# One transformer layer with experts on one core: TensorE transposes for batch 0, weight loads one head ahead, a ring of one-row gathers, a running sum on VectorE, and batch 1 prepared later

## The chip, the cores and the metric

The kernel runs on one core of a Trainium2 chip. The core has five engines, each with its own instruction queue: PE (TensorE, matmuls), DVE (VectorE), ACT (ScalarE), POOL (GpSimd) and SP (SyncE, which here only issues DMAs). POOL issues DMAs as well. The engines wait for each other and for DMAs through semaphores; within one queue, instructions start in order. The time is the device time of one execution in microseconds.

## The reference

There are B = 4 sequences of S = 512 rows with D = 512 columns. A small cross attention is added first, then a layer with causal attention of 16 heads and a mixture of experts (top 6 of 16, 352 wide) with a shared expert (704 wide).

```python
# cross attention: the keys and queries come from ctx, the values are layernorm(x)
query = einsum('bnc,dc->bnd', ctx, Wq) + bq ; key = einsum('bnc,dc->bnd', ctx, Wk) + bk
attention = softmax(einsum('bnd,bmd->bnm', query, key))
x = x + einsum('bln,bmn->blm', layernorm(x), attention)
# the layer, on hidden = layernorm(x)
h = rmsnorm(hidden, ln1_w); q, k, v = h @ wq, h @ wk, h @ wv      # 16 heads of 128
attn = softmax(causal(q k^T / sqrt(128)))
x1 = hidden + (attn v) @ wo
t = rmsnorm(x1, ln2_w)
probs = softmax(t @ gate_w.T); topv, topi = top_k(probs, 6); topv /= sum(topv)
routed = sum over the six of topv * (silu(t @ eg_w) * (t @ eu_w)) @ ed_w
shared = (silu(t @ sg_w.T) * (t @ su_w.T)) @ sd_w.T
out = x + layer output, where the layer output is x1 + routed + shared
```

## The kernel before

Most products are made of three fp16 products. `split` (lines 72 to 74) makes a high half with ACT (L73) and the rest, the low half, with DVE (L74); `mm3` (L80 to 88) issues hi by hi, hi by lo and lo by hi into one PSUM bank (source lines L83, L86, L87). A product of two fp32 operands thus costs three matmuls and two splits. PSUM has eight banks, given out by tag: "a" three, "s" three, "w" two.

`flip` (L90) is a DMA transpose issued on SP. It turns the normalised cross attention (`pn` into `ptp`, for `xm`) and the normed rows (`hh` into `hT`, for queries, keys and values), 128 rows at a time. `after` (L93) makes one instruction stand behind another on its queue, without a wait of its own on the chip. Apart from these, a scheduler decides the order of each queue from the program order, the dependences and its own timing model.

*The cross attention* of batch b is the generator `xattn(b)` (L204 to 363). It loads the context, x and its transpose (batches 0 and 1 on SP, later ones on POOL), and then yields between small steps: projections `xq`, energies `en`, softmax (`pm`, then split into `pn`), `flip` into `ptp`; `stats` (L250) for the row norms, `center` (L266), which subtracts the mean on POOL; per row tile the product `xm`, its addition to the centred rows (L337), the statistics of the result, its power -1/2 on POOL (L347), `hu`, the split `hh`, and `flip` into `hT`. A call of `step(b, n)` runs n steps. The driver (L370 to 390) runs batch 0 to its end, then the loads of ln2 and of the gate, then nine steps of batch 1. Where PE would stand idle in batch 0, `warm` fills it with 22 matmuls that nobody reads.

*The attention* runs over a list of 64 pairs (batch, head), in groups of two heads (HG = 2): four heads of batch 0, then groups of batches 0 and 1 by turns, so that two batches share a loaded weight, and then the same with batches 2 and 3. In each turn of the loop (L780 to 841) head n is prepared (`queries`, `values`, then `scores`), and the head one turn behind is finished (`attend`: the softmax goes through a flip `pt` on SP, then `av`; `project`: `wo` and the residual). Steps of the next batch's cross attention are issued in between, for batch 1 two in each of the first six turns. For the first head `queries` and `values` first run on half of the rows (L790 to 794), since the first half of `hT` lands earlier.

*Weights* come through `fetch` (L407 to 434). At first use the fp32 weight is loaded into a staging tile (`wqk_st`, `wv_st`, `wo_st`; two buffers), split by ACT and DVE, used, and its fp16 form written to DRAM at once (L429). In later batches the fp16 form is loaded (L414) when the head is issued. These DMAs are on POOL, except for the first ones.

*The routing* of a batch (`route2`, L532) has softmax, top 6 and, over the 16 experts, a running sum in four doublings (L578 to 582), with the copies on DVE and the additions on POOL. `scatter` (L456 to 475) writes rows into expert order, 96 indirect DMAs on POOL (L467), paced by `pace`, a copy on POOL that waits for an attention result.

*The experts* (L1119 to 1219) run one by one: gate and up (`g`, `u`), `hf` and its low half on DVE, down (`y`), and a store `y_d`. As soon as rows have all six results, POOL gathers them (L1169) and DVE adds them, weighted, to `acc` (L1178). The gathered rows land in a tile `yg` of three rows, of which there are two; `lookahead(tile, 3, 4)` (L1197) sets this up, with up to four gathers kept in flight. Before the last stage `gather_all(0)` (L1212) waits until none is in flight, and further tiles are taken from another pool.

## Time and profile before

| what | us |
|---|---|
| runs | 1768.77, 1769.27, 1786.13 |
| median of the runs | 1769.27 |
| the profiled execution | 1762.41 |
| its span | 1760.7 |
| PE busy | 1708.6 |
| DVE, ACT, POOL busy | 1116.2, 829.3, 485.1 |

The profiled execution took 6.9 us less than the median. The span is the part from the first to the last recorded event. PE is busy in 97% of it. Three views are needed to read it: the list of an engine's waits, with what ended them; a queue's timeline, one line to an instruction or a run of like ones, with the idle time ahead of it in brackets; and windows, one line to a stretch, with each engine's busy time and instruction count, the granted TensorE clock (1.00 is full speed), the DMA share and the rate.

The page's list of DMA issues gives the time from issue to landing, for instance:

```profile
y_d<-yt SPq DMA_DIRECT2D x96, 256.0 KB, 2.8
wqk<-wqk_d POOLq DMA_DIRECT2D x20, 512.0 KB, 5.0
wqk_d<-wqk POOLq DMA_DIRECT2D x15, 512.0 KB, 4.0
wqk_st<-in_wqk_dram POOLq DMA_DIRECT2D x14, 512.0 KB, 6.4
```

The columns are the transfer, the queue, its count, the size of one, and the median time to landing.

### The profile page before, as it was taken

Reading aid. Unit: us, or ns where it says so; the run is one execution under the profiler, and the core shown is the slowest. Engines: PE = TensorE matmul, PEld = TensorE weight load, DVE = VectorE, ACT = ScalarE, POOL = GpSimd, SP = SyncE. Lnnn points to the kernel's source line nnn. Section 1 sums busy time; section 2 is a strip of 40 time slices with the busy share of each in tenths; the row PEclk is TensorE's granted clock in tenths of the full one; section 3 lists DMA queues with packets and bytes.
Section 4 is the critical chain, followed back from the end, with each engine's and each line's share of the span. In section 5 each row is a group of like instructions: output and inputs, shape, how many; then the busy total and the mean of one; then the engine's idle time right before and its main releaser. Section 6 shows DMA issues by size and latency. Waiting matters only on the chain. (4 is left out here: it accounts for less than half of the span.)

```text
span 1760.7 us, 27659 instructions
## 1 busy us (share of the span) xinstructions
PE 1708.6 (97%) x9919; PEld 932.9 (53%) x9919; DVE 1116.2 (63%) x2766; ACT 829.3 (47%) x1711; POOL 485.1 (28%) x614
## 2 busy tenths in 40 slices
PE   7899999999998999999999999999999999999998
PEld 3555556565654555556555544455555555555553
DVE  6787877787785676776667647544434344356755
ACT  4565655565643545454445422344544445444431
POOL 5524212240255242121113454300000000034654
PEclk9999999999999999999999999999999999999999
DMA  7787867575687787556547653755554546589866
GB/s 246 181 205 184 225 150 192 122 196 118 138 183 187 163 177 179 120 120 118 111 104 132 140 155 128 247 173 148 150 173 137 154 143 163 154 228 254 221 198 213
DMA packets 392212, 296.24 MB, mean 168 GB/s; under 512 B 334880, under 2 KB 335136, under 8 KB 391296
## 3 DMA queue, kind: packets, MB, share of 16 engines
q1 hardware_dynamic: 353360, 159.87, 39.9%
q0 software_dynamic: 38704, 134.51, 25.5%
q8 instruction: 80, 1.31, 0.3%
q14 instruction: 68, 0.56, 0.1%
HBM read 124.81 MB, written 88.94 MB: 121 GB/s over the span
## 5 line engine op out<-in xcount | busy, mean ns | idle before, releaser
L1169 POOL DMA_INDIRECT yg<-y_d,yrc x96 | 109.9, 1145 | 505.2 <-PE u L87 426.0
L673 ACT ACTIVATE pe<-pe,bnm 128x128 f32<-128x128 f32 (+3 forms) x256 | 142.5, 557 | 161.5 <-DVE bnm L671 161.3
L83 PE MATMUL qk<-hT,wqk 128*128 128x512 f16 (+1 forms) x520 | 196.4, 378 | 9.1 <-DMA wqk<-wqk_d 5.5
L86 PE MATMUL qk<-hT,wqk 128*128 128x512 f16 (+1 forms) x520 | 196.5, 378 | 0.0
L87 PE MATMUL qk<-hT,wqk 128*128 128x512 f16 (+1 forms) x520 | 196.3, 377 | 0.0
L74 DVE SCALAR_TENSOR_TENSOR pn<-pe,brc,pn 128x128 f16<-128x128 f32 (+3 forms) x256 | 148.1, 590 | 21.3 <-ACT pn L73 18.0
L671 DVE CUSTOM_DVE_ANT_0 pe<-sc,causal 128x128 f32<-128x128 f32 (+3 forms) x256 | 117.0, 485 | 66.9 <-PE sc L668 65.9
L73 ACT ACTIVATE pn<-pe,brc 128x128 f16<-128x128 f32 (+3 forms) x256 | 133.5, 553 | 34.1 <-ACT pe L673 17.8
L83 PE MATMUL v<-wv,hT 128*128 128x256 f16 x512 | 139.8, 273 | 0.9 <-DMA hT<-hh 0.9
L87 PE MATMUL v<-wv,hT 128*128 128x256 f16 x512 | 139.7, 273 | 0.0
L86 PE MATMUL v<-wv,hT 128*128 128x256 f16 x512 | 139.7, 273 | 0.0
L83 PE MATMUL g<-xT,wt 128*128 128x384 f16 (+2 forms) x384 | 127.3, 331 | 0.0
L86 PE MATMUL g<-xT,wt 128*128 128x384 f16 (+2 forms) x384 | 127.2, 331 | 0.0
L87 PE MATMUL g<-xT,wt 128*128 128x384 f16 (+2 forms) x384 | 127.2, 331 | 0.0
L1058 ACT ACTIVATE hT_e<-hf 128x384 f16<-128x384 f32 (+3 forms) x96 | 51.1, 532 | 133.6 <-DVE hf L1072 133.2
L83 PE MATMUL y<-dt,hT_e 128*128 128x512 f16 (+1 forms) x288 | 109.4, 380 | 0.0
L87 PE MATMUL y<-dt,hT_e 128*128 128x512 f16 (+1 forms) x288 | 108.9, 378 | 0.0
L86 PE MATMUL y<-dt,hT_e 128*128 128x512 f16 (+1 forms) x288 | 108.9, 378 | 0.0
L73 ACT ACTIVATE qkt<-qk 128x512 f16<-128x512 f32 x128 | 75.1, 587 | 70.7 <-PE qk L87 70.5
L705 DVE SCALAR_TENSOR_TENSOR x<-wo,x 128x512 f32<-128x512 f32 x128 | 87.2, 685 | 33.3 <-PE wo L87 32.9
L467 POOL DMA_INDIRECT xs_d<-h2p,slotu x96 | 98.7, 1028 | 28.3 <-issue 27.1
L74 DVE SCALAR_TENSOR_TENSOR qkt<-qk,qkt 128x512 f16<-128x512 f32 x128 | 87.5, 684 | 18.3 <-ACT qkt L73 15.2
(333 smaller groups left out, 4041.5 us busy)
## 6 DMA issues: line engine op xcount, KB each, us to landing
y_d<-yt SPq DMA_DIRECT2D x96, 256.0 KB, 2.8
est<-in_ew_dram SPq DMA_DIRECT2D x32, 704.0 KB, 6.2
est<-in_ed_dram SPq DMA_DIRECT2D x16, 768.0 KB, 4.7
wqk<-wqk_d POOLq DMA_DIRECT2D x20, 512.0 KB, 5.0
wqk_d<-wqk POOLq DMA_DIRECT2D x15, 512.0 KB, 4.0
wqk_st<-in_wqk_dram POOLq DMA_DIRECT2D x14, 512.0 KB, 6.4
xs_d<-causal POOLq DMA_DIRECT2D x16, 384.0 KB, 5.6
wv<-wv_d POOLq DMA_DIRECT2D x10, 512.0 KB, 5.7
```

What stands on the lines that cost most here:

```text
L73: return (nc.scalar.activation(hi, src, AF.Copy, scale=scale), nc.vector.scalar_tensor_tensor(lo, src, scale, hi, ALU.mult, ALU.subtract))
L74: nc.vector.scalar_tensor_tensor(lo, src, scale, hi, ALU.mult, ALU.subtract))
L83: ins = nc.tensor.matmul(o, lh, rh, start=start and j == 0, stop=False)
L86: nc.tensor.matmul(o, lh, rl, start=False, stop=False)
L87: ins = nc.tensor.matmul(o, ll, rh, start=False, stop=stop and j == n - 1)
L467: ins = nc.gpsimd.indirect_dma_start(out=xs_d, out_offset=bass.IndirectOffsetOnAxis(ap=slotu[:, tt, k:k + 1], axis=0), in_=h2ps[tt], in_of ...
L671: nc.vector.tensor_tensor_reduce(pe, ps[:, :w], causal[:, S - w:], -1.0, 3e38, ALU.add, ALU.min, nm)
L673: nc.scalar.activation(pe, pe, AF.Exp, bias=nm, scale=-1.0, accum_out=sm)
L705: nc.vector.scalar_tensor_tensor(x2[:, t, :], ps, 1.0 / (VS * WS), x2[:, t, :], ALU.mult, ALU.add)
L1058: nc.scalar.activation(hT[:R, ic, :w], hf, AF.Copy)
L1169: nc.gpsimd.indirect_dma_start(out=yg, out_offset=None, in_=src, in_offset=bass.IndirectOffsetOnAxis(ap=idx[:, tt, k:k + 1], axis=0))
```

## The change

1. *Transposes.* A new helper `swap` multiplies four 128x128 blocks of the high half by an fp16 identity (`id16`) into one PSUM bank, then four of the low half into another; ACT copies the first bank out, and DVE (for `ptp`) or ACT (for `hT`) the second. Batch 0 uses it in place of `flip`. Batches 1 to 3 keep `flip`.
2. *Batch 0's start.* x is loaded ahead of its transpose. `center` is on ACT for batch 0. `warm` issues 12 matmuls in place of 22. The first two `xm` products are computed in four column pieces, each as soon as its part of `ptp` is there; the other two take "s" banks. The driver stops batch 0 after eleven steps; the rest of it (`second_half`: its last two row tiles, the loads of ln2 and gate, five steps of batch 1) comes after the first half of the first head. The second head's weight `wqk1` is fetched there too.
3. *Batch 1.* It goes on by four steps in each of the first six turns, except turn 1, in place of two. Its transposed x (`xT32`) is loaded into the "wo" buffers of the weights and not into the staging buffers.
4. *Weights.* In each turn the loads of the next head's fp16 weights (`wqk`, `wv`, and `wo` after `attend`) are issued at the end of the preparation, if the weight has been seen before. Write-backs are kept in a list and issued behind the staging load of a later weight. `pace` also stands behind the last such load.
5. *Running sum.* The four additions go to DVE.
6. *Gathers.* A ring of seven tiles of one row, with five gathers kept in flight, takes the place of two tiles of three. The `hs` tiles of the shared expert get a pool of their own, which closes before the experts; the last batch's lie in the experts' weight staging. The call before the last stage has no argument, so it doesn't wait for gathers in flight.

```diff
+    def swap(o, i, tag, low):
+        done = []
+        for a, put in enumerate((nc.scalar.copy, low)):
+            ps = bank(tag, "swap")
+            for c in range(C):
+                j = (a * C + c) * P
+                nc.tensor.matmul(ps[:, c * P:(c + 1) * P], i[:, j:j + P], id16, start=True, stop=True)
+            done.append(put(o[:, a * C:(a + 1) * C, :], ps.rearrange("p (c q) -> p c q", c=C)))
+        return done
...
-            t = (stg if b else wg).tile([P, 1024], F32, tag="st" if b else "wo", name="xT32")
+            t = (stg if b > 1 else wg).tile([P, 1024], F32, tag="st" if b > 1 else "wo", name="xT32")
...
+            if b == 0:
+                zz["center"] = nc.scalar.activation(xt[:, t, :], xt[:, t, :], AF.Identity, bias=nb[:, t:t + 1])
+                after(zz["center"], zz["calm"][0])
+                return
             nc.gpsimd.tensor_scalar(xt[:, t, :], xt[:, t, :], nb[:, t:t + 1], None, ALU.add)
...
-            zz["ptp", b] = flip(ptp[:, :, ml], pn)
+            if b:
+                flip(ptp[:, :, ml], pn)
+            else:
+                zz["third"] = zz["calm"][1] if m else None
+                zz["calm"] = swap(ptp[:, :, ml], pn, "a", nc.vector.tensor_copy)
...
-            warm(22, last)
+            warm(12, last)
...
+        early_xm = [bank("w", f"xm{b}_{t}") for t in range(0 if b else 2)]
+        for m in range(NT):
+            ml = slice(m * P, (m + 1) * P)
+            for t, ps in enumerate(early_xm):
+                tl = slice(t * P, (t + 1) * P)
+                zz["xm", b, t] = mm3(ps[:, ml], [(lnp[:, c, tl], lnp[:, C + c, tl], ptp[:, c, ml], ptp[:, C + c, ml])
+                                                 for c in range(C)])
+        if b == 0:
+            early_xm += [product(t, "s") for t in range(2, NT)]
...
-            zz["hT", b] = flip(hT[b][:, :, tl], hh)
+            if b:
+                flip(hT[b][:, :, tl], hh)
+            else:
+                zz["cast"] = swap(hT[b][:, :, tl], hh, "as"[t // 2], nc.scalar.copy)[1]
...
-    step(0, 99)
+    step(0, 5 + 6)
...
+    def second_half():
+        step(0, 99)
+        after(zz["low", "wqk1"], zz["hh", 0])
...
+        step(1, 5)
...
-    step(1, 1 + 2 * NT)
...
+        w = soon.pop(nm, None)
+        if w is None:
+            w = pool.tile([P, 2, n], F16, tag=tag, name=f"{nm}_{b}")
+            if nm in seen:
+                zz["load"] = nc.gpsimd.dma_start(w.rearrange("p a n -> p (a n)"), scr)
+        if early:
+            soon[nm] = w
+            return
...
+            save(0, None if nm == "wqk1" else ins)
...
+    def save(keep, behind=None):
+        while len(unsaved) > keep:
+            scr, w = unsaved.pop(0)
+            zz["pad"] = nc.gpsimd.dma_start(scr, w.rearrange("p a n -> p (a n)"))
+            if behind:
+                after(zz["pad"], behind)
...
-            nc.gpsimd.tensor_tensor(nx[:, :, sft:], cs[:, :, sft:], cs[:, :, :E - sft], ALU.add)
+            nc.vector.tensor_tensor(nx[:, :, sft:], cs[:, :, sft:], cs[:, :, :E - sft], ALU.add)
...
+            if n + 1 < NH:
+                b, h = heads[n + 1]
+                wqk_of(b, h, True)
+                if h % HG == 0:
+                    wv_of(b, h // HG, True)
...
+                wo_of(b, h // HG, True)
...
-            step(1, 2)
+            step(1, 4 * (n != 1))
...
-    lookahead(lambda: st2.tile([P, 3, D], F32, tag="hs", name="yg"), 3, 4)
+    hctx.close()
+    ring_p = ctx.enter_context(tc.tile_pool(name="ring", bufs=RING, side="right", reuse_waits="tile"))
+    lookahead(lambda: ring_p.tile([P, 1, D], F32, name="yg"), 1, RING - 2)
...
-    gather_all(0)
+    gather_all()
```

## The prediction

> **What bounds the kernel now.** I read the page's busy shares first, then what TensorE (PE) waited for, then the timelines of the queues that feed each wait.

> ```profile
> PE 1708.6 (97%) x9919; PEld 932.9 (53%) x9919; DVE 1116.2 (63%) x2766; ACT 829.3 (47%) x1711; POOL 485.1 (28%) x614
> ```
> ```profile
> PE av L83 <- DMA pt<-pn: 16.9, 10, 3.9
> PE xm L83 <- DMA ptp<-pn: 9.8, 2, 5.8
> PE qk L83 <- DMA wqk<-wqk_d: 5.5, 1, 5.5
> PE u L1081 <- DVE hf L1072: 3.9, 2, 2.1
> PE qk L83 <- DMA hT<-hh: 3.6, 2, 3.2
> ```
> The columns are total us, times, longest. PE is the bound: of a span of 1760.7 us it lacks 52.1. The change leaves the products alone, so it can only take from these 52.1 us, from matmuls run at a lower clock, and from the few matmuls that it adds or drops. The listed waits make 39.7 of the 52.1; smaller ones and some 8 us behind the last matmul are the rest.

> ```profile
> 25.64 0.58 PE L83 MATMUL xm<-ptp,lnp 128*128 128x512 f16 x1 [5.82 <-DMA ptp<-pn]
> 26.02 0.63 PE L86 MATMUL xm<-ptp,lnp 128*128 128x512 f16 x1
> 26.45 0.63 PE L87 MATMUL xm<-ptp,lnp 128*128 128x512 f16 x1
> ...
> 548.81 0.61 PE L83 MATMUL qk<-hT,wqk 128*128 128x512 f16 x1 [5.51 <-DMA wqk<-wqk_d]
> 549.21 0.63 PE L86 MATMUL qk<-hT,wqk 128*128 128x512 f16 x1
> 549.64 0.63 PE L87 MATMUL qk<-hT,wqk 128*128 128x512 f16 x1
> ...
> 1626.41 0.32 PE L1081 MATMUL u<-xT,wb 128*128 128x384 f16 x1 [2.13 <-DVE hf L1072]
> 1626.57 0.32 PE L1082 MATMUL u<-xT,wb 128*128 128x384 f16 x1
> ```
> Columns: start, us, engine, line, operation, the idle time before it and what ended it. Behind the waits of 5.82 and 5.51 us the 512-column matmuls follow each other every 0.43 us; elsewhere it is 0.2155. This lasts some 3.2 us, so such a wait costs about 1.6 us more. Behind the 2.13 us there is no such stretch. The granted clock says the same by window:

> ```profile
> 540.00:560.00 20.00, 14.49 (x75) 7.54 (x74) 9.10 (x28) 6.36 (x16) 9.39 (x13) 0.83 0.75 172
> 560.00:580.00 20.00, 20.00 (x126) 11.95 (x125) 13.37 (x36) 7.80 (x18) 9.37 (x13) 1.00 0.90 220
> ```
> Last, the queues behind the waits:
> ```profile
> 16.77 7.28 SPq L91 DMA_TRANSPOSE ptp<-pn  x4
> 24.16 8.16 POOL L267 TENSOR_SCALAR xt<-xt,nb 128x512 f32<-128x512 f32 x4 [0.88 <-DVE nb L262]
> 538.93 0.96 POOL L467 DMA_INDIRECT xs_d<-h2p,slotu  x1 [0.30 <-issue]
> 539.89 0.60 POOL L414 DMA_DIRECT2D wqk<-wqk_d  x1
> 150.91 0.22 PE L666 MATMUL sc<-qkt,qkt 128*128 128x128 f16 x1
> 150.97 0.22 PE L667 MATMUL sc<-qkt,qkt 128*128 128x128 f16 x1
> ```

> **The change part by part.** All sums are against the profiled execution, 1762.41 us, of which 1760.7 is span; the median shown is 1769.27, 6.9 above it, and I carry the saving over to the median unchanged. "Work" is PE time counted at full clock in queue order (0.2155 us for 512 columns, pro rata below).

> 1. Swaps in batch 0. Eight tiles by eight 128-column matmuls are 64; the two `sc` lines above follow each other by 0.054 to 0.06 us: 64 x 0.054 = 3.45 us. Ten warm matmuls go: -2.16. Net +1.29 of PE. [...]

> 2. The start of batch 0. Before, the four flips end at 24.05, the first `xm` starts at 25.64, POOL centres rows until 32.32, and the first `v` starts at 40.74. After, each `ptp` part waits for its PSUM copies; three DVE copies at about 0.6 (the ScalarE copy of 128x512 from PSUM is 0.59) put the last at about 24. The first two `xm` need only their last quarter then (24 matmuls of 0.054), so they are there at 25.3, all four by 30.5. Centring on ACT starts at 26.3 (`nb` behind POOL's power and two staged splits) and takes four times about 0.6. DVE then has for two row tiles: xt 1.3, statistics 1.2, small ones 0.6, hu 1.3, hh 1.4: from 26.9 to 32.8. Swap and copy add 1.2 to 1.7: first `v` at about 34.5. Rows 2 and 3 follow by the same list at 42.5, where before `hT` landed at 51.32. Then `xq1` waits for the low half of the next context (DVE, about 47), and `qk0_1_0` starts at about 52.1 with 38.4 of work done: 13.7 lost. Before it starts at 58.89 with 39.65 done: 19.2 lost. Difference 5.5, less the 1.29: **-4.2**. Moving x's load ahead of xT's is booked at nothing: ACT reads xT behind 10.82; 0 to +1.

> 3. Batch 1 a step later. `xm1_0` has 77 us of work ahead of it in place of 53, and its four flips stand on SP long before: the wait of 3.97 at 76.60 and its slow stretch go, **-5.6**. Small waits around it (0.67, 0.25) go too, -0.9. In exchange, work between the last `xm1` and the first `qk1_4` falls from 10.67 to 8.41. In the trace that chain (DVE list, POOL's power, hh, flip) took 11.25, with 0.39 waited; by DVE's order after it is about 9.0 of DVE and 3.1 from hh to landing, 12.1. So 3.7 are waited, 3.3 more. Here the clock decides: the trace has half clock after 3.23 and none after 2.48. [...] I take the rows: 1.6, together **+4.9** (0 to +6). What is late is queued as follows: on PE everything behind `qk1_4_0` stands.

> 4. Heads. The room between a head's last `sc` and its `av` falls for av1_5 from 17.0 to 12.5 us of work, for av0_13 from 16.6 to 13.7, rises for av1_1 from 9.2 to 11.8, and falls for av1_3 from 11.2 to 9.6. The waits of 1.58 (av1_1) and 2.48 (av1_3) so trade places: 0, with -6 to +4. Batches 2 and 3 keep theirs. (Room is counted in both queue orders, as work is.)

> 5. Weight loads ahead. The load that PE awaited at 548.81 was issued at 539.89, behind ten scatters; in the new order it precedes all of them. 5.51 and 1.5 of slow matmuls go: **-7.0** (-4 if it lands late by the wait of its buffer). Most other loads keep their place in POOL's order. Write-backs behind the staging loads: nothing waits for them but later batches, 0.

> 6. Running sum on DVE: four adds a batch, 0.15 to 0.4 us each by the small DVE rows; PE has heads in front of it there and waits for no route: 0 (0 to +1).

> 7. Ring of seven rows. The two waits of `u` for `hf` (DVE held by an add whose row was late, 1.95 at 1623.47) sum to 3.9; a gather now waits for the add seven rows back, before at times four. I book **-3.5** (-4 to 0). Changed `hs` buffers and the last stage without its drain: PE never waits there, 0.

> Sum: -4.2 - 5.6 - 0.9 + 4.9 - 7.0 - 3.5 = **-16.3**: 1746.1 for the profiled execution, 1753.0 for the median.

> **The rivals.** *All of it comes.* `hT` of batch 1 lands in time, as in the trace within 0.39: 5 less, and av waits in batches 0 and 1 (1.90, 1.58, 2.48) vanish: 6 less; 1742 to 1748. For it: the trace chain held beside a busier DVE. Against: 2.3 us of cover are gone.

> *Given back.* The start of batch 0 moves only from DMA to DVE and ACT, whose copies and splits I placed from lists and not from a trace: part 2 gives 0, and the hT wait is 5: 1760 to 1765. For it: DVE is 13.5 to 16 of 20 us busy there already.

> *Slower: ACT held by staged weights.* POOL issues 29 staging loads (14 `wqk`, 8 `wo`, 7 `wv`), landing in about 6 us. ACT already waits 26.1 us for them (9.9, 9.2 and 7.0 by its list of waits), up to 3.78 at 175.67; a softmax held there shows as the 1.90 of av1_5. With less room (part 4) and heads starting 10 us earlier the whole 26.1 could reach PE: 24 more, 1777. From 16.3 of the 26.1 on, the kernel is slower than before. Against it: so far 1.9 of it arrives, and batch 1's xT leaves the staging buffers. [...]

> That the change doesn't do what it says holds in part: the loads "ahead" mostly wait for the same buffers. If the one at 548.81 does too, 1760.

> **How the numbers follow.** Forecast 1753 (1748 to 1760): 0.45. All comes: 0.25. Given back: 0.18. Slower: 0.12, half of it beyond 1%. One per cent, 17.7 us, is about what a measurement of this kernel can tell from no change; it lies at 1751.6, inside the forecast's own range, of which I put 0.17 below. Faster 0.25 + 0.17 = 0.42; slower 0.06; within 0.52. The range leaves out the slower rival and the last of the gains: 1740 to 1767.

> **What would show it.** First `v` near 34.5 and `qk0_1_0` near 52; no wait of `xm` for `ptp`; no wait for `wqk_d`; a new wait of `qk1_4` for `hT` of 3 to 4 us with half clock behind it; `u` without waits for `hf`. The forecast is wrong if waits for `hT` or `pt` sum to more than 25, or if swaps follow each other at over 0.1 us.

## The result, and the profile after

The changed kernel takes 1794.38 us (median; 1782.19 to 1796.64), the kernel before beside it 1772.14. The ratio is 1.0138 [1.0104, 1.0172]: about 24 us slower by the ratio (22 by the medians), where 16 less were forecast. Two later series of the same kernel gave 1.0056 [1.0031, 1.0082] and 1.0119 [1.0076, 1.0163]. The sign holds in all three; the size is anything from 10 to 24 us.

The busy shares of the changed kernel (busy us, share of the span, instructions):

```profile
PE 1721.8 (96%) x10045; PEld 942.0 (53%) x10045; DVE 1124.0 (63%) x2787; ACT 835.3 (47%) x1727; POOL 487.5 (27%) x594
```

PE is 13.2 us busier than before, yet the 126 matmuls that were added are short ones (64 swaps; `xm` in quarters; ten warm ones fewer). Counted by columns at full clock, PE's work is 1678.1 us against 1676.8, the 1.3 more that the prediction booked. Most of the rest of the busier PE is half clock: by the distance between back-to-back matmuls 22.7 us go to it, 14.2 before. The remainder of the span is waiting. What PE waited for, in the changed kernel (total us, times, longest):

```profile
PE av L84 <- DMA pt<-pn: 21.9, 8, 7.0
PE qk L84 <- DMA hT<-hh: 8.8, 1, 8.8
PE u L1167 <- DVE hf L1158: 7.6, 3, 5.4
PE xq L84 <- DVE vt L75: 7.0, 1, 7.0
PE swap L99 <- ACT hh L74: 2.9, 1, 2.9
PE wo L84 <- DVE x L774: 2.2, 1, 2.2
```

Two of the old waits are gone, `xm` for `ptp` (9.8) and `qk` for `wqk_d` (5.5). Three are new: `hT` at 8.8, `xq` for `vt` at 7.0, and a wait of `av` for `pt` of 7.0, where the longest was 3.9. (A second one of 5.5, at 98.5, was only 1.9 and 2.3 in the two later executions.) On the timeline of PE (start, us, engine, line, operation, idle before and what ended it):

```profile
150.41 0.61 PE L84 MATMUL qk<-hT,wqk 128*128 128x512 f16 x1 [8.79 <-DMA hT<-hh]
150.81 0.63 PE L87 MATMUL qk<-hT,wqk 128*128 128x512 f16 x1
...
381.69 0.58 PE L84 MATMUL xq<-ctp,wxp 128*128 128x512 f16 x1 [7.01 <-DVE vt L75]
382.06 0.63 PE L87 MATMUL xq<-ctp,wxp 128*128 128x512 f16 x1
...
604.23 0.61 PE L84 MATMUL av<-pt,vt 128*128 128x512 f16 x1 [7.02 <-DMA pt<-pn]
604.62 0.63 PE L87 MATMUL av<-pt,vt 128*128 128x512 f16 x1
```

Each is followed by matmuls 0.4 us apart, that is by half clock. The windows of these waits show it beside the DMA engines (window, its length, then busy us and count of PE, PEld, DVE, ACT and POOL, granted clock, DMA share, GB/s):

```profile
141.40:150.40 9.00, 0.23 (x4) 0.05 (x1) 3.33 (x7) 2.44 (x5) 1.91 (x3) 0.76 0.98 192
150.40:153.60 3.20, 3.19 (x8) 1.19 (x9) 2.47 (x4) 0.00 (x0) 0.00 (x0) 0.50 1.05 326
374.70:381.70 7.00, 0.01 (x1) 0.01 (x1) 4.46 (x10) 0.00 (x0) 0.00 (x0) 0.75 0.58 28
...
597.20:604.20 7.00, 0.01 (x1) 0.00 (x0) 1.47 (x7) 1.05 (x4) 2.77 (x3) 0.70 1.02 270
```

In the first and the last stretch PE stands while the DMA engines are full (shares of 0.98 and 1.02). In the middle one, at 0.58, it stands while they are not: there, DVE is what is late.

**Where each stage lost its time.** A head's start in the two kernels is no fair comparison, since steps of other batches have moved across it. So I added up, from PE's records, 0.2155 us per 512 columns for every matmul issued so far, and took the sum from the clock. What is left is the time that PE lost, idle or at half clock. (The whole work comes out the same in every execution of a kernel, so no records are missing.) Heads are counted from 0 in the order in which their `av` starts; the last stage begins behind the last `y`. "Before" has two profiled executions (the second is e16 below), "changed" three (the result, e0, e12); the last two columns are experiments, explained below.

| stage, us lost | before | changed | mean difference | e4 | e17 |
|---|---|---|---|---|---|
| to `qk0_1_0` | 19.2, 17.9 | 16.2, 16.0, 15.1 | -2.8 | 15.7 | 15.1 |
| to head 0 | 5.7, 7.1 | 1.1, 1.0, 1.3 | -5.3 | 1.0 | 3.7 |
| heads 0 to 18 | 5.6, 12.9 | 23.2, 17.4, 19.0 | +10.6 | 10.4 | 16.4 |
| 18 to 19 | 0.1, 0.1 | 8.9, 8.0, 7.1 | +7.9 | 3.5 | 1.2 |
| 19 to 29 | 4.5, 5.5 | 5.9, 13.2, 8.9 | +4.3 | 11.0 | 11.7 |
| 29 to 34 | 11.4, 7.2 | 11.4, 9.4, 11.7 | +1.5 | 7.5 | 3.1 |
| 34 to 63 | 16.5, 10.0 | 13.7, 11.1, 13.8 | -0.4 | 14.8 | 12.2 |
| to the last stage | 12.2, 12.2 | 19.3, 8.6, 9.2 | +0.2 | 13.8 | 11.2 |
| last stage | 1.0, 5.6 | 8.6, 1.1, 8.7 | +2.8 | 1.0 | 8.7 |

The mean differences sum to 18.9 us; with 1.3 more of work and 0.4 less behind the last matmul this is the 19.8 by which the mean spans differ (1781.4 and 1761.65). Two readings matter. Up to head 63 the changed kernel loses 76.1 to 80.3 us in each of its executions and the kernel before 60.7 to 63.0: that is the change, some 16 us. Behind head 63 both kernels vary from one execution to the next by more than they differ. The loss sits in heads 0 to 29, and the stage 29 to 34, where 7 us were to be won, gives nothing.

### The profile page after: what moved, and what is told of

Its sections match the earlier page's. It is cut to its first block, busy times and chain, and to the rows that moved or that the text cites. A ratio compares the mean times of both kernels' runs of the same rounds, so it can differ in the third digit from the quotient of the medians.

```text
span 1793.4 us, 27893 instructions
## 1 busy us (share of the span) xinstructions
PE 1721.8 (96%) x10045; PEld 942.0 (53%) x10045; DVE 1124.0 (63%) x2787; ACT 835.3 (47%) x1727; POOL 487.5 (27%) x594
## 5 line engine op out<-in xcount | busy, mean ns | idle before, releaser
L1255 POOL DMA_INDIRECT yg<-y_d,yrc x96 | 120.5, 1255 | 507.9 <-DMA y_d<-yt 424.7
L87 PE MATMUL qk<-hT,wqk 128*128 128x512 f16 (+1 forms) x520 | 196.5, 378 | 0.1
L74 ACT ACTIVATE pn<-pe,brc 128x128 f16<-128x128 f32 (+3 forms) x256 | 133.6, 552 | 19.7 <-ACT pe L742 13.7
L87 PE MATMUL v<-wv,hT 128*128 128x256 f16 x512 | 140.4, 274 | 0.6 <-issue 0.6
L87 PE MATMUL g<-xT,wt 128*128 128x384 f16 (+2 forms) x384 | 127.2, 331 | 0.0
L87 PE MATMUL y<-dt,hT_e 128*128 128x512 f16 (+1 forms) x288 | 109.3, 380 | 0.0
L536 POOL DMA_INDIRECT xs_d<-h2p,slotu x96 | 100.7, 1049 | 28.1 <-issue 26.9
```

The costliest lines, as they stand in the source:

```text
L74: return (nc.scalar.activation(hi, src, AF.Copy, scale=scale), nc.vector.scalar_tensor_tensor(lo, src, scale, hi, ALU.mult, ALU.subtract))
L87: nc.tensor.matmul(o, lh, rl, start=False, stop=False)
L536: ins = nc.gpsimd.indirect_dma_start(out=xs_d, out_offset=bass.IndirectOffsetOnAxis(ap=slotu[:, tt, k:k + 1], axis=0), in_=h2ps[tt], in_of ...
L1255: nc.gpsimd.indirect_dma_start(out=yg, out_offset=None, in_=src, in_offset=bass.IndirectOffsetOnAxis(ap=idx[:, tt, k:k + 1], axis=0))
```

## The experiments

The theories, as the runs treat them. First: the flip of `hT` for batch 1 and the 1 MB load of x for batch 2 meet on the DMA engines, since the later batch 1 put them side by side. Second: batch 3's x is late on POOL's queue, and DVE stands at its statistics. Third (G, where a letter is used): the ring of gathers is to blame, in the experts. The rival to them all (O): these are only places where a common shortage shows, so that one wait removed brings another. Each ratio is to runs of the kernel before on the same chip.

**e0, e1, e2: the changed kernel again; its loads not ahead; its old gathers** (one chip).

```diff
 e1, in fetch
-        if early and nm not in seen or soon.get(nm) and early:
+        if early:
 e2
-    lookahead(lambda: ring_p.tile([P, 1, D], F32, name="yg"), 1, RING - 2)
+    lookahead(lambda: hsp.tile([P, 3, D], F32, tag="hs", name="yg"), 3, 4)
-    gather_all()
+    gather_all(0)
```

> The changed kernel once more, for a second profile. Theory C (collision: loads that the change moves beside flips make PE wait 5.5 us at 98, 8.8 at 150, 7.0 at 381 and 7.0 at 604, each with about 1.6 us of half clock): the same four waits within 2 us each, time 1.010 to 1.017 of before. Rival V (such waits fall where they like from one execution to the next): two or more of the four are gone and others stand elsewhere. Rival G (the expert stages: the 5.4 of u for hf at 1650 and the 6.5 us lost behind 1745): both are there again.

> The changed kernel with weight loads issued when the head is issued, as before. Theory C: the 7.0 us of av for pt at 604 goes, since the two loads ahead of its flips stand later; the wait of qk for wqk of 5.5 at about 550 comes back, so the time stays within 0.3% of the changed kernel. Rival: loads ahead only gain, then 7 us slower (0.4%).

> The changed kernel with two gather tiles of three rows, four gathers in flight and the drain before the last stage, as before. Rival G: the 5.4 at 1650 and the last stage's 6.5 us go, 10 to 13 us faster (0.6 to 0.7%). Theory C: those were not of the ring's making, within 3 us of the changed kernel.

e0: 1.0056 [1.0031, 1.0082]. Its list of waits:

```profile
PE av L84 <- DMA pt<-pn: 18.7, 9, 6.0
PE qk L84 <- DMA hT<-hh: 8.8, 1, 8.8
PE xq L84 <- DVE vt L75: 6.2, 1, 6.2
```

The three new waits are there again, at nearly the same size, while no wait of `u` for `hf` and no "issue" is listed. So what belongs to the change lies before the experts.

e1: 1.0100 [1.0076, 1.0123]. Without loads ahead the changed kernel is 0.44% slower, 7.8 us by the ratios (3.8 by the medians, 1783.82 and 1780.04; the intervals just overlap). They are not the loss. Nor is this the gain that was forecast. In e1's one profiled execution (the longest of 21) the wait for `wqk` doesn't come back, and POOL shows why:

```profile
551.72 0.53 POOL L466 DMA_DIRECT2D wqk<-wqk_d  x1 [0.58 <-PE qk L88]
...
557.12 1.13 POOL L536 DMA_INDIRECT xs_d<-h2p,slotu  x1 [0.18 <-DVE x L774]
```

The load stands ahead of the scatters although it is no longer issued a head ahead. `av` waits for `pt` twice there, 9.9 and 13.6 us, where one such wait was expected to go.

e2: 1.0067 [1.0039, 1.0095], the same as e0. The ring neither costs nor saves a measurable time, and with that the third theory falls.

**e3: batch 1 by four steps in every turn** (turn 1 too; the same chip).

```diff
-            step(1, 4 * (n != 1))
+            step(1, 4)
```

> The changed kernel with batch 1's four steps in turn 1 too, so that batch 1 ends one turn sooner. Theory C: the wait of qk for hT at 150 (8.8 and half clock after it) goes, 8 to 11 us faster (0.5 to 0.6%). Rival: the wait only moves on to av in batch 0 (flips of ptp and pt stand closer), less than 3 us.

0.9977 [0.9944, 1.0009]. The wait in front of batch 1's first `qk` fell to 2.84 (listed as "issue"; the flip still takes 8.2, but more work covers it), the wait of `xq` went, and `xm` for `ptp` came back with 3.76. This looked like the answer, and was not (e13).

**e4, e5, e6, e7: the flip and the load of x kept apart** (another chip). e4 issues x's load only when `hT` is there, by a one-element copy on POOL that reads `hT`; e5 is e4 with e3's edit. e6 makes the last row tile of batch 1 by `swap`, with no flip. e7 is e3 with each write-back issued at once, as in the kernel before.

```diff
 e4 (and e5, with step(1, 4))
+        if b > 1:
+            nc.gpsimd.tensor_copy(xt[0:1, 0, 0:1].bitcast(F16)[:, 0:1], hT[b - 1][0:1, 2 * C - 1, S - 1:S])
 e6
-            if b:
+            if b > 1 or b == 1 and t < 3:
                 flip(hT[b][:, :, tl], hh)
 e7 (with step(1, 4))
+            save(0)
```

> The changed kernel; the loads of x for batches 2 and 3 (1 MB) stand behind a copy of one element from the last columns of the batch before's hT, so they start when that flip has landed. Theory C (the flip takes 8.8 us because the x load is issued 0.02 us behind it): the flip lands in about 3 us, the wait of qk for hT falls from 8.8 to 3 to 4 us, 5 to 7 us saved there; x lands some 4 us later, so xq's wait for vt (6.2) grows by 0 to 4: in all 2 to 7 us faster than the changed kernel (1.002 to 1.0045 of before on this scale, from 1.0056). Rival L (the flip is late for another reason, such as the flips of pt ahead of it on the queue): the wait stays within 1 us of 8.8.

> Both: batch 1's four steps in each turn, and x behind hT. Theory C: the 2.8 us of qk in front of batch 1's first head (139.7) goes, the rest as with four steps in each turn; 0.993 to 0.998 of before. Rival L: no difference from four steps in each turn (0.998), or slower by the later x.

> The changed kernel with batch 1's last hT tile transposed by TensorE (eight matmuls and two ScalarE copies) and not by a flip. Theory C: no DMA stands in front of batch 1's first qk; from hh (9 us of DVE list after xm) swap and copies take 1.5 us, wait 1 to 3 us in place of 8.8, so 7 to 9 us faster with the half clock. Rival L (DVE's list is the long part): 2 us faster at most.

> Batch 1's four steps in each turn, and each weight's fp16 copy written to DRAM at once and not behind the next staging load. If the deferred write-backs give staging loads room, the waits of av for pt in batches 0 and 1 grow by 3 to 10 us here; if they only move traffic, within 3 us of four steps in each turn (0.998).

For the first theory, SP's queue in the changed kernel:

```profile
141.44 1.26 SPq L92 DMA_TRANSPOSE hT<-hh  x1
```

and POOL's:

```profile
141.46 0.84 POOL L226 DMA_DIRECT2D xt<-in_x_dram  x1 [0.30 <-POOL x L386]
```

The flip and the load go out within 0.02 us, and PE's first `qk` follows the flip by 8.97 (150.41 above). In e4, SP's queue:

```profile
136.27 1.26 SPq L92 DMA_TRANSPOSE hT<-hh  x1
```

POOL's:

```profile
140.07 0.80 POOL L228 DMA_DIRECT2D xt<-in_x_dram  x1 [0.32 <-POOL xt L227]
```

and PE's:

```profile
139.45 0.61 PE L84 MATMUL qk<-hT,wqk 128*128 128x512 f16 x1 [2.99 <-DMA hT<-hh]
139.85 0.63 PE L87 MATMUL qk<-hT,wqk 128*128 128x512 f16 x1
```

With the load held back, `qk` follows the same flip by 3.18. Up to that `qk`, PE, DVE, ACT and SP run the same instructions in the same order in e0 and e4; only on POOL has the load moved. So it is the load of x that made it 9. Over all kernels that have this flip, by the place of the load:

| load of x issued | kernels | flip to first `qk` of batch 1, us |
|---|---|---|
| 4.8 behind the flip | e5 | 4.1 |
| 3.8 behind | e4, e10 | 3.2 |
| 0.83 behind | before, e16 | 3.1 |
| 0.5 behind | e7, e17 | 5.9 to 6.1 |
| 0.02 behind | changed, e0, e1, e2, e8, e12 | 8.7 to 9.2 |
| 0.27 ahead | e3, e9, e13, e14 | 8.1 to 8.7 |
| 0.40 ahead | e11 | 10.8 |

In the kernel before, the load goes out 0.83 us behind the flip, and the flip lands as if alone. The wait of 2.99 that stays in e4 is what the forecast meant: the flip alone is 3.1, with half clock behind it.

Yet the times: e4 1.0048 [1.0020, 1.0076], e5 1.0046 [1.0021, 1.0072], e6 1.0054 [1.0031, 1.0077], e7 1.0006 [0.9983, 1.0029]. The changed kernel itself was not run on this chip, on which the kernel before takes 1761.87 against 1766.17 on that of e0 to e3; so whether e4 to e6 gain on it stays open. They don't reach the kernel before, and e5 and e6 miss what was expected of them. What came in exchange shows in e6, first on POOL:

```profile
543.11 0.96 POOL L536 DMA_INDIRECT xs_d<-h2p,slotu  x1 [0.30 <-issue]
544.08 0.60 POOL L466 DMA_DIRECT2D wqk<-wqk_d  x1
```

then on PE:

```profile
557.12 0.61 PE L84 MATMUL qk<-hT,wqk 128*128 128x512 f16 x1 [8.93 <-DMA wqk<-wqk_d]
```

The load of `wqk` is behind ten scatters again, as in the kernel before, and PE waits 8.93 for it. In e0, POOL had it ahead of all of them (545.39, and the first scatter at 550.78), as in e1 above.

Editing batch 1, some 400 us earlier, had moved the order in which the scheduler puts the two. The wait returned in e4 (3.92), e5 (4.27), e8 (4.16), e9 (5.13) and e10 (4.59) as well. Where it doesn't and write-backs are deferred, `av` waits for `pt` some 45 us later: 7.02, 5.97 and 5.87 in the changed kernel, 3.0 to 9.5 in e2, e3, e11, e13, e14 and e15. The gain of the prediction's part 5 thus hangs on a position that nothing in the code fixes; e1 has it without the early loads.

**e8, e9, e10: batch 3's x and DVE; e11: flips in batch 0** (a third chip). For the second theory, POOL's queue in the changed kernel:

```profile
362.65 0.60 POOL L222 DMA_DIRECT2D xT<-in_xT_dram  x1 [3.75 <-DVE bnm L740]
...
365.18 0.78 POOL L226 DMA_DIRECT2D xt<-in_x_dram  x1
```

and DVE's:

```profile
377.24 0.69 DVE L266 BATCH_NORM_STATS2 st<-xt 128x6 f32<-128x512 f32 x1 [7.64 <-DMA xt<-in_x_dram]
...
380.97 0.66 DVE L75 SCALAR_TENSOR_TENSOR vt<-v,vt 128x512 f16<-128x512 f32 x1
```

The load of x stands 2.5 us behind that of xT and lands 12.1 behind its issue. In the kernel before, x's load went first (347.55, ahead of 352.14) and took 7.8. DVE stands 7.64 us at the statistics of x; the low half of `vt` is queued behind them, and for it PE waited 7.01 (381.69). e8 sets the statistics behind the last split of `xq`, where they hold nothing up; e9 is that with e3's edit; e10 is it with e4's. e11 takes the flips back into batch 0; what was ordered behind a swap's copies is there ordered behind the split ahead of it.

```diff
 e8 (e9 with step(1, 4), e10 with e4's copy)
+                else:
+                    after(ins, zz["xqk", b])
...
-            nc.vector.tensor_tensor(t[:, 1], qf, t[:, 0], ALU.subtract)
+            zz["xqk", b] = nc.vector.tensor_tensor(t[:, 1], qf, t[:, 0], ALU.subtract)
 e11
-            if b:
-                flip(ptp[:, :, ml], pn)
-            else:
+            flip(ptp[:, :, ml], pn)
...
-                zz["calm"] = swap(ptp[:, :, ml], pn, "a", nc.vector.tensor_copy)
+                zz["calm"] = zz["sm", 0]
...
-            if b:
-                flip(hT[b][:, :, tl], hh)
-            else:
-                zz["cast"] = swap(hT[b][:, :, tl], hh, "as"[t // 2], nc.scalar.copy)[1]
+            flip(hT[b][:, :, tl], hh)
+            if b == 0:
+                zz["cast"] = both[0]
```

> The changed kernel; on VectorE the row statistics of x for batches 2 and 3 stand behind the last xqk of their batch, so VectorE does not wait for the x load. Theory S (VectorE stands 6.5 us in front of batch 3's statistics for an x that lands late, and what is queued behind it, vt, holds PE): the wait of xq for vt (6.2, with half clock behind it) goes, 6 to 8 us faster than the changed kernel (about 1.001 to 1.002 of before); the wait of qk for hT stays at 8.8. Rival: PE then waits as long for en or sc of the same heads, less than 3 us.

> Batch 1's four steps in each turn, and the statistics behind. There VectorE waits for x only 5.2 us in two and PE not at all for it, so theory S expects no more than 3 us: 0.996 to 0.999 of before. Rival (order by itself moves other waits): outside of 0.993 to 1.003.

> The changed kernel with x behind hT and the statistics behind: both causes away. Theories C and S together: the 8.8 (to about 3) and the 6.2 go, with half clock 12 to 17 us in all, 0.996 to 0.999 of before. Rival O (each new order brings a wait of its own elsewhere, as the wait for wqk at 555 that came back with x behind hT): 1.002 to 1.006.

> The changed kernel with DMA flips in batch 0 too, the rest of its new start kept. If the swaps bring the start's gain (av of the first head is 5.1 us earlier than before in the changed kernel), the first av comes 4 to 8 us later than in the changed kernel: 1.008 to 1.010 of before. Rival: the order of the start, not the swaps, brings it: within 2 us of the changed kernel at the first av.

e8: the wait of DVE for x and that of `xq` are both gone, and 18 to 19 loses 3.4 us in place of 7.1 to 8.9. The mechanism is as told. But e8 takes 1.0122 [1.0077, 1.0167], e9 1.0133 [1.0075, 1.0192] and e10 1.0116 [1.0070, 1.0162]: in e8 `av` waits for `pt` 7.08 at 101 and 5.53 at 192.5, in e10 5.26 at 98 and 6.50 at 186, and `wqk` is late again in all three. The wait near 100 was in the changed kernel too (5.5 in one execution, 1.9 and 2.3 in two); that near 190 was not. e10, which removes both of the waits for x, is no faster than e8: up to head 63 it loses 74.8 us, e8 82.5, the changed kernel 76.1 to 80.3, and it loses 32.9 behind head 63. So part of what was removed came back elsewhere, as the rival said. These three have four runs each.

e11: 1.0275 [1.0199, 1.0350]. Up to `qk0_1_0` it loses 27.8 us, the changed kernel 15.1 to 16.2; less the 3.4 of work that the swaps are, and with the rest of the new start in place, the swaps and the order that hangs on them are worth some 8.5 us there. The first `av` comes at 96.6 and not at 80.2 to 81.0: 16 us, where 4 to 8 were expected.

**e12 to e15: the changed kernel a third time, and e3 again** (a fourth chip). e13 is e3's kernel. e14 gives turn 1 two steps; e15 is e3's edit with e6's.

```diff
 e14
-            step(1, 4 * (n != 1))
+            step(1, 2 if n == 1 else 4)
```

> The changed kernel, to stand beside the next three on one chip. 1.005 to 1.015 of before; waits of qk for hT at about 145 to 150 of 8.6 to 9.0 us and of xq for vt at about 375 to 382 of 3 to 7 us.

> Batch 1's four steps in each turn. If batch 1's place is the cause of the loss: 0.6 to 1% faster than the changed kernel beside it, no wait for hT above 4, none of xq for vt. If the first comparison was the chip's: within 0.3% of it.

> Two steps of batch 1 in turn 1, between none (changed) and four. Work between the last xm1 and the first qk1_4 is 10.7 us as before the change (8.4 in the changed kernel), and xm1 stands at 68 us of work (77 changed, 53 before). If lateness is the cause: wait for hT 4 to 6 us less than in the changed kernel, and the wait of xm for ptp (3.8 to 4.9 with four steps) is as large as with four: time like four steps in each turn within 0.3%. If the order as a whole decides: anywhere from 0.995 to 1.01 of before.

> Four steps in each turn, and batch 1's last hT tile by TensorE. No wait in front of batch 1's first qk (2.8 to 3.0 there with the flip): 3 us faster than four steps in each turn, if the order of the rest stays; with the load of wqk behind the scatters again (a wait of 4 to 9 at 555), 1 to 6 us slower.

e12: 1.0119 [1.0076, 1.0163]. Its list of waits:

```profile
PE av L84 <- DMA pt<-pn: 19.1, 10, 5.9
PE qk L84 <- DMA hT<-hh: 8.6, 1, 8.6
PE xq L84 <- DVE vt L75: 4.3, 1, 4.3
PE sg L88 <- issue: 3.3, 2, 2.0
```

The same three waits; the "issue" waits of the last stage are back and those of `u` are not.

e13: 1.0111 [1.0062, 1.0161]. The same program had given 0.9977 as e3, so e3's gain doesn't hold. Its profile has `pt` at 9.54 and `u` at 4.64. e14: 1.0103 [1.0065, 1.0141], no help, though its wait for `hT` is 5.83. e15: 1.0060 [1.0033, 1.0087]: without the flip of the last row tile it is 0.5% faster than e13 beside it, about 9 us by the ratios (3.6 by the medians; the intervals overlap). The stages don't give this to the flip: of the lost time 4 us less lie in heads 0 to 18 and 11.5 less in 29 to 34, and 5.6 more in 18 to 19, where `xq` waits 4.2 for `vt` again, which no one expected.

**e16, e17: the kernel before, and e7 again** (the fourth chip).

> The kernel before, for a second profile. If the added waits are the change's: wait of qk for hT in front of batch 1 under 1 us, none of xq for vt, wait of av for pt at about 585 of 2 to 4; the wait of xm for ptp twice (5.8 and 4.0) and that of qk for wqk (5.5) again; 1.000 of itself. If they come and go with the execution: one of them over 4 here too.

> Batch 1's four steps in each turn and each fp16 copy written at once, a second time, beside the kernel before. If it is as fast as before: 0.997 to 1.004. If the first comparison was the chip's: 1.006 to 1.012, as four steps in each turn on the second chip.

e16: 0.9984 [0.9956, 1.0011]. Its list of waits has no `vt`, no wait above 5.5, and `pt` at most 2.2:

```profile
PE av L83 <- DMA pt<-pn: 16.0, 11, 2.2
PE xm L83 <- DMA ptp<-pn: 10.1, 2, 5.5
PE qk L83 <- DMA hT<-hh: 3.7, 2, 3.3
PE qk L83 <- DMA wqk<-wqk_d: 3.3, 1, 3.3
```

The new waits are the change's then, not the execution's. e17: 0.9992 [0.9969, 1.0015], as e7 level with the kernel before, and 1.2% below e13, from which it differs by the write-backs alone, with intervals well apart. But e3, the same program as e13, was level with both, so the times alone don't settle it. With write-backs at once, x's load for batch 3 is ahead of xT's again (350.36 and 354.77 in e17), and 29 to 34 loses 5.2 (e7) and 3.1 (e17), where e3 and e13 lose 8.3 and 17.5: `av` waits 2.38 and 1.29 for `pt` there, not 6.01 and 9.54. (All waits of `av` for `pt` sum to 17.0 in e7 and 15.1 in e3, so neither outcome expected of e7 came as written.) From 18 to 19 the four lose 1.2 to 1.6, so e3's edit alone is enough against that wait; with e6's beside it (e15) it isn't. No version beat the kernel before by more than the noise.

## Why the prediction was wrong

The step that failed is a group of three that were booked at nothing: "Batches 2 and 3 keep theirs" (part 4), "Write-backs behind the staging loads: nothing waits for them but later batches, 0" (part 5), and, inside part 3, the landing of `hT`, taken from a flip that no load met. I costed what the moved instructions do on their own engines. I did not ask which large transfers they would now stand beside, or behind what they would queue. In their place the runs showed, in the three executions, a wait of 8.6 to 8.8 us for `hT`, one of 4.3 to 7.0 for `vt` and one of 5.9 to 7.0 for `pt`. The prediction by stage, against the mean differences of the table:

| stage | forecast | measured | term |
|---|---|---|---|
| to `qk0_1_0` | -5.5 | -2.8 | start of batch 0 (lost time; the 1.29 of swaps is work) |
| to head 0 | -6.5 | -5.3 | waits of `xm1` |
| heads 0 to 18 | +4.9 | +10.6 | `hT` of batch 1 |
| 18 to 19 | 0 | +7.9 | x of batch 3 |
| 19 to 29 | 0 | +4.3 | small waits, one by one |
| 29 to 34 | -7.0 | +1.5 | `wqk` ahead, `pt` |
| 34 to 63 | 0 | -0.4 | |
| experts and last stage | -3.5 | +3.0 | ring; varies by execution |

1. *Swaps*: right. Twelve of them take 0.83 us in a row (at 17.42 in the changed kernel), so they follow each other by 0.055 us, as the `sc` rows had it, and the work grew by the 1.3 us booked.

2. *Start of batch 0*: right in kind, and short. First `v` came at 36.09 (forecast 34.5), `qk0_1_0` at 54.54, 54.41 and 53.5 (52.1). What was missing is a wait of the first `swap` for `hh`, and half clock behind it. PE's timeline in the changed kernel:

```profile
33.80 0.61 PE L99 MATMUL swap<-id,hh 128*128 128x128 f16 x4 [2.91 <-ACT hh L74]
```

and PE in windows around it (length, busy us and count, granted clock, DMA share, GB/s):

```profile
30.02:33.43 3.41, 0.87 (x5) 1.00 0.87 326
33.43:36.85 3.42, 2.81 (x20) 0.50 0.02 7
36.85:40.26 3.41, 3.41 (x18) 0.50 0.44 154
```

I had summed PE's idle time there without asking in how large a piece it falls.

3. *Batch 1 a step later*: the waits of `xm1` went as forecast. For `hT` the mechanism was right and the size was not: a wait of 3.7 and 1.6 of slow matmuls were booked, 8.6 to 8.8 and 2.1 to 2.9 measured, some 6 more. e4 shows both halves: with x's load held back the wait is 2.99 and the slow matmuls cost 1.2. The 1.6 was itself a short reading: behind the 5.51 at 548.81 in the kernel before, half clock lasted to 554.0 and cost 2.6; the 0.83 of the window shown there is 6.8 us of half clock in 20. The range given, "0 to +6", took in a late DVE and no transfer. The view that would have told was POOL's queue at 136.59 in the kernel before, where x's load goes out 0.83 us behind the flip: any step that delays batch 1 alone closes that gap.

4. *Heads*: wrong. The `av` of head 33 waited 7.02, 5.97 and 5.87 in the changed kernel, 2.48 and 1.42 in the kernel before. It waits for the last of its four flips, and this flip is slow in both:

| kernel | work from last `sc` to `av` | of it behind the last flip's issue | that flip lands after | wait |
|---|---|---|---|---|
| before, e16 | 11.15 | 5.33 | 8.05, 6.99 | 2.48, 1.42 |
| changed, e0, e12 | 9.64 | 1.08, 2.64, 0.00 | 8.26, 8.78, 6.04 | 7.02, 5.97, 5.87 |
| e3, e13 | 9.64 | 2.75 | 8.95, 12.46 | 6.01, 9.54 |
| e7, e17 | 12.93 | 6.25 | 8.85, 7.71 | 2.38, 1.29 |

So it is not the flip that changed but the work that covers it: the room fell by 1.5 us, where batches 2 and 3 were to "keep theirs", and the flip goes out later in it. SP's queue shows one reason, in the changed kernel and then in e17:

```profile
591.00 0.34 SPq L782 DMA_DIRECT2D acc<-r_d  x1
591.51 10.45 SPq L92 DMA_TRANSPOSE pt<-pn  x6
...
579.64 2.88 SPq L92 DMA_TRANSPOSE pt<-pn  x2
583.11 0.34 SPq L783 DMA_DIRECT2D acc<-r_d  x1
584.74 1.25 SPq L92 DMA_TRANSPOSE pt<-pn  x1
```

In the changed kernel all four flips stand behind the load of `acc`, which goes out 3.5 us behind the end of the last `sc` (1.2 ahead of it in the kernel before); in e17 two are ahead of it. Write-backs at once give the longer room in e7 and e17, by the scheduler's order; no run separates this from the queue on SP. The 7.9 us of 18 to 19, booked under "keep theirs", came from batch 3's x: in each kernel with deferred write-backs its load is behind that of xT, in each with write-backs at once (before, e7, e16, e17) ahead of it. It needs `vt` behind it on DVE as well: e8 and e3 take that away, in different ways, and most of the 7.9 goes.

5. *Loads ahead*: the wait for `wqk` is gone, as forecast, but not shown to be the early loads' doing: in e1, without them, the load is still ahead of the scatters. That e1 is slower by 7.8 us, by the ratios, for a forecast of 7.0 is luck, since in its profile it loses by other waits. And the stage gains nothing, because the wait for `pt` 45 us behind takes the room.

6 and 7. *Running sum*: no sign of a cost. *Ring*: not confirmed; e2 without it is as fast, and `u` waited for `hf` 7.6, nothing and 0.3 in the three executions.

The rival on the slower side had the right sign and another cause. The waits of ACT for staged weights, which were to grow by 16 us to decide, sum to 26.1 and 30.9 in the two executions of the kernel before and to 31.2, 30.4 and 33.4 in the changed one. The loss came through flips and loads that land late for their place, which the prediction touched only as a limit to watch ("waits for `hT` or `pt` sum to more than 25"): they sum to 30.7, 27.5 and 27.7, after 21.4 in the kernel before.

What stays open: why the same program differs by up to 1.3% against the kernel before from one series to the next (e3 and e13); most of the losses of 19 to 29, of which one recurs (`wo` waits 2.2, 3.2 and 1.8 us for DVE's x near 520, 0.2 before); and the experts and the last stage, where the changed kernel lost 27.9, 9.7 and 17.9 us in three executions and the kernel before 13.2 and 17.8. No run tells a cause for these. Of e3 and e13, the profiled executions lose 56.9 and 72.3 us up to head 63, and 9 of the difference lie in 29 to 34, where the same flip lands after 8.95 and 12.46.

## What to carry to other kernels

When a step is moved, list the large loads that it will now go out beside, on every queue, with the gap between issues before and after: here a transpose that takes 3 us took 9 because it and a 1 MB load, once 0.8 us apart, went out together. A position in a queue that only a scheduler's model gives is not a gain that one can keep; fix it in the code, or expect it to flip with the next edit. And when one wait is removed and the time doesn't fall, count lost time by stage over several executions of both kernels before believing any one cause.

## What the runs showed of the hardware

In these kernels PE's first `qk` follows the issue of a DMA transpose of one row tile of `hT` by 3.1 us with a 1 MB load 0.83 us behind it (before, e16), and by 3.2 with the load 3.8 behind (e4); by 6 with the load 0.5 behind (e7, e17); and by 8 to 9 with both at once or the load 0.27 ahead (changed, e3). Under a microsecond of order decides 6 us here.

```profile
581.36:584.77 3.41, 1.59 (x8) 1.00 1.12 280
584.77:588.19 3.42, 2.76 (x18) 1.00 1.10 308
```

In the last stage PE shows, in some executions, pieces of about 1 us in which it waits for nothing that the profile shows. In e12 the longest is

```profile
1739.88 0.38 PE L88 MATMUL sg<-h2T,shw 128*128 128x512 f16 x1 [1.97 <-issue]
```

They sum to 4.9 us there, to 3.6 in the first execution of the changed kernel and to 1.6 in e16, the kernel before. They don't follow the kernel: the eight profiles of e0 to e7, on two chips, have none there, and the ten of e8 to e17, on two others, all have them, the changed kernel being among both (e0, e12). Their cause was not tried.
